# Norm products in bank pairs of their own, and a shared end of the last convolution chunk: four layers on one Trainium2 core

## The chip, the cores and the metric

One core of a Trainium2 chip runs the whole program. The metric is the device time of one execution in microseconds (us). The engines are called PE (TensorE's matrix products; PEld are its weight loads), DVE (VectorE), ACT (ScalarE), POOL (GpSimd) and SP (which here only issues transfers).

## The reference

The input is x of shape 4 x 256 x 56 x 56 in 32-bit floats. Four layers follow, each of the form x = x + layer(gn(x)); gn is a normalization over 32 groups of eight channels.

- Layer 0 is an involution: a 1x1 product to 64 channels and a second one to 49 x 16 make a 7x7 kernel for each pixel and each group of 16 channels, and that kernel is applied to the group.
- Layer 1 is a residual block of two 3x3 convolutions with batch norms and relu.
- Layer 2 is an involution again, with batch norms and relu inside.
- Layer 3 multiplies gn(x) with the sum of two gates: one per channel (a sigmoid of a 256x256 product; the sum over the transformed plane is the first pixel), and one per pixel (the real part of the 2-D Fourier transform of the channel mean, the "map" below).

## The kernel before

Work goes by units: an image b and a block cb of 128 channels, eight units in each involution. Layer 3 is fused into layer 2's involution; layer 1 runs between, in 12 chunks of 16 to 20 rows. The order on each engine is the order in which the Python code emits instructions (`in_order` fixes it). Work for other units is hung into the loops as generators, advanced at numbered places: `hooks` (after round n of the tap stage) and `late` (after column tx).

A unit has a tap stage and seven columns.

- `tap_matrices`: 32 rounds, each with six products (L613) into one pair of PSUM banks, read by DVE (L634, two rounds of three) or ACT (L627) into `kt`.
- `apply`, one call for each column: 20 + 36 products (L659) into two pairs, which ACT (L672 or L674) and DVE (four L679) sum; POOL (L684, layer 0) or DVE (L686, layer 2) adds the sum onto the image. After it, seven transposes (L427) make the next windows in a third pair, ACT copies them (L439), and SP shuffles them by transfers (L445, L446). POOL (L412) or ACT (L410) normalizes the next strip.

The pairs come from one pool of four, in rotation: a new pair waits until the readers of the one four allocations before are done. There is also `spare[0]`, a free part of a pair that is in use. It was set in the tap stage and in `apply`, where the second pair uses only its first bank:

```
pair = two_banks()
spare[0] = pair[:, 1, :]
```

`norm_steps` makes the factors of a group norm from statistics, in nine steps: the aggregate (L215), a product with a group-averaging matrix (L226), a copy and three small operations (L229 to L237), a second product (L240), the root (`rsqrt_eps`: L150 on DVE, L151 on POOL) and the shift (L244). In layer 0 the next image's norm runs between columns, its products into `spare[0]`; so does one norm in layer 2's first unit (the last image's).

`bottleneck` is the 1x1 product: first a small product (L467) whose result becomes a bias `hb` (L478 in layer 2, on DVE), then L489 into several pairs, which ACT reads with that bias (L508) into `hp`, with copies on DVE (L497). For layer 2's first image it stands in front of everything, so PE's first L613 there needs all L508.

The convolutions work on transformed columns, in the order k = 1, 2, 3, 4, 0, 5 (`KS`). `filtered_product` makes an inner and an outer pair of products (L1606) and DVE sums them (L1618 to L1624); L1810 to L1813 and `middle` (L1633, L1634) mix the columns. `joined` ends a chunk: L1752 adds the scaled result onto the normed residual. In the last chunk (i = 11), DVE also does relu and the residual sum (L1757) for both channel blocks, then SP stores them. In the chunk before it (i = 10), ACT does the relu (L1764) and a transfer on POOL accumulates the residual (L1765) before the store (L1766). The statistics of the last image are DVE's `bn_stats` (L1784), six for each of these two chunks: those of chunk 10 stand inside chunk 11, those of chunk 11 at hook 3 of layer 2's first tap stage. For earlier images they are ACT's passes over the chunk (`mean_of`, `spread_of`: L1771, L1772, L1777, L1778).

After the last column, the last image's end follows: `warm` issues idle products (L340) while DVE finishes; `last_mean` makes channel means by 28 products (L913) with the last norm between them; `last_gates` makes the map (L939, L949, L952) with DVE's L947 between, spreads it into rows (L962), and for each of seven chunks multiplies it back to all partitions (L972), followed by two L975 on DVE, two L976 on ACT and two stores. `last_ones` (L852) makes the constant tables for this with reductions of an identity matrix.

Of the kernel before, what the change touches and what calls it, by code (L numbers as in the profile page):

```python
# [12 lines left out]
ALU = mybir.AluOpType  # L13
# [60 lines left out]
def net_kernel(  # L74
# [243 lines left out]
    def involution_layer(layer, xin, xout, red, span, sb, xs_of, ahead=None, pending=None):  # L318

        with ExitStack() as es:  # L320
# [130 lines left out]
            def bottleneck(b):  # L451
# [23 lines left out]
                if layer == 0:  # L475
                    nc.vector.tensor_add(hb, ps[:, 0:1], by_row(L0_RB))
                else:
                    nc.vector.scalar_tensor_tensor(hb, ps[:, 0:1], bn["s3"], bn["t3"], ALU.mult, ALU.add)  # L478
                yield
# [166 lines left out]
            def apply(b, cb, kt, tx, xw):  # L646
# [3 lines left out]
                for ng, tys, nty, rows in O_PARTS:  # L650
                    pair = two_banks()
                    spare[0] = pair[:, 1, :]
                    nb, m = len(tys), ng * GC
                    v = pair[:, :nb, : ng * nty * TP].rearrange("p i (e n) -> p i e n", e=ng)
                    for i in range(nb):
                        for k in range(nty):
                            ty = tys[i] + k
                            for j in range(P // m):
                                nc.tensor.matmul(  # L659
                                    v[m * j : m * j + m, i, :, k * TP : (k + 1) * TP],  # L660
                                    xw[:, window(ty), m * j : m * j + m],
                                    kt[:, ng * j : ng * j + ng, :, ty * NTX + tx, :],
                                    start=True,
                                    stop=True,
                                )
                    n = rows // nb * TX
                    o = [v[:, :, e, :n] for e in range(ng)]
                    un = work.tile([P, 2, O_PARTS[0][3] // 2 * TX], F32, name="un")
                    un = un.rearrange("p i n -> p (i n)")[:, : rows * TX]
                    part = un.rearrange("p (i n) -> p i n", i=nb)  # L670
                    if layer == 0:
                        nc.scalar.mul(part, o[0], bn["par"][ng][:, 0:1])  # L672
                    else:
                        nc.scalar.activation(  # L674
                            part, o[0], AF.Identity, bias=bn["t4"][:, cb : cb + 1], scale=bn["s4"][ng][:, 0, cb : cb + 1]
                        )
                    for e in range(1, ng):
                        s = bn["par"][ng][:, e : e + 1] if layer == 0 else bn["s4"][ng][:, e, cb : cb + 1]
                        nc.vector.scalar_tensor_tensor(part, o[e], s, part, ALU.mult, ALU.add)  # L679
                    dst = img[:, y0 : y0 + rows, tx * TX : (tx + 1) * TX]  # L680
                    y0 += rows
                    u = un.rearrange("p (r x) -> p r x", x=TX)
                    if layer == 0:
                        nc.gpsimd.tensor_tensor(dst, u, dst, ALU.add)  # L684
                    else:
                        nc.vector.scalar_tensor_tensor(dst, u, 0.0, dst, ALU.max, ALU.add)  # L686
# [160 lines left out]
            def last_ones():  # L847

                by = ident_sb[:, : CR * CR]
                for i, axes in enumerate(("p (j r) -> p r j", "p (j r) -> p j r")):  # L850
                    last_xn[i] = dead(B - 1, NB - 1, 6 * CR * W + 128 + i * CR, CR)
                    nc.vector.tensor_reduce(last_xn[i], by.rearrange(axes, r=CR), mybir.AxisListType.X, ALU.add)  # L852

# [80 lines left out]
            def last_gates(b):  # L934
# [13 lines left out]
                ps = one_bank()  # L948
                nc.tensor.matmul(ps[:H, :W], half, cs2_sb, start=True, stop=False)  # L949
                for i in range(4):  # L950
                    e, c = divmod(i, 2)
                    nc.tensor.matmul(  # L952
                        ps[:H, :W], down[: H // 2, e, c], part[:, e, c], start=False, stop=(i == 3)
                    )

# [4 lines left out]

                rows = dead(b, NB - 1, 2 * CR * W, CR * W)[:H]
                nc.vector.tensor_tensor(  # L962
                    rows.rearrange("y (r w) -> y r w", r=CR),
                    ps[:H, :W].unsqueeze(1).to_broadcast([H, CR, W]),
                    last_xn[0][:H].unsqueeze(2).to_broadcast([H, CR, W]),
                    ALU.mult,
                )
                nc.vector.scalar_tensor_tensor(back, shift, -1.0, inv, ALU.mult, ALU.mult)
                for j in range(NCHUNK):
                    at = slice(j * CR * W, (j + 1) * CR * W)  # L970
                    sf = one_bank()[:, : CR * W]
                    nc.tensor.matmul(sf, last_xn[1][:H, j : j + 1].to_broadcast([H, P]), rows, start=True, stop=True)  # L972
                    for cb in range(NB):
# [14 lines left out]
            def norm_of(layer, sts, u0, u1):  # L988
                return norm_steps(sts, lambda: spare[0], layer, u0, u1)

            hooks0 = {}
            if layer == 0:
                place(hooks0, begin(), (1, 2, 4, 6, 7))
            else:
# [4 lines left out]
                run(bottleneck(0))  # L999
                hooks0[3] = list(pending[0])  # L1000
                for _ in range(NXW - 1):
                    next_windows()
                    next_strip()
                hooks0[7] = [next_windows, next_strip]
            if layer == 0:
                next_strip()
# [36 lines left out]
            for u, (b, cb) in enumerate(units):  # L1043
# [24 lines left out]
                if b + 1 < B:  # L1068
                    n = 16 if layer == 0 else (26, 21)[cb]
                    hooks.setdefault(n, []).append(load_step(b + 1, cb))  # L1070

                last_image = layer == 0 and b == B - 1
                if last_image and cb == 0:
# [11 lines left out]
                if b + 1 < B:  # L1085
                    if layer == 0:
                        g = sums(b + 1, cb)
                        if cb == 0:
# [3 lines left out]
                            def norm_first():  # L1092
                                yield from norm_of(0, {u + 2: sums_of[b + 1, 0]}, u + 2, u + 3)

                            g = norm_first()
                            for tx in (3, 4, 4, 4, 4, 4, 5, 5, 6):
                                late[tx].append(step(g))
                        else:
# [3 lines left out]
                            def norm_last():  # L1102
                                yield from norm_of(0, {u + 2: sums_of[b + 1, 1]}, u + 2, u + 3)

                            g = norm_last()
                            late[1].append(step(g))
                            late[2] += [step(g)] * 5
                            late[3] += [step(g)] * 3
# [15 lines left out]
                if last_image and cb == 0:  # L1124
                    g = norm_of(1, {}, 0, u)
                    for tx in (1, 2, 2, 2, 2, 2, 3, 3, 4):
                        late[tx].append(step(g))
                if layer == 2 and u == 0:
                    g = norm_of(2, dict(enumerate(pending[1], NB * (B - 1))), NB * (B - 1), NB * B)
                    for tx in (1, 2, 2, 2, 2, 2, 3, 3, 4):  # L1130
                        late[tx].append(step(g))
# [30 lines left out]
            if layer == 2:  # L1162
                run(last_normed(b, 0))
                bank = one_bank()
                mean, norm = last_mean(b, bank), by_counts(norm_steps({u: st}, lambda: bank, 3, u, u + 1), (1, 1, 4, 1, 1, 1))
                warm(16, ident_sb)
                for _ in range(2):
# [53 lines left out]
    def conv_layer(xin, xout, st, ahead):  # L1221
        with ExitStack() as es:
# [474 lines left out]
            def conv2(i, after, between, sums, tail):  # L1697
# [28 lines left out]
                def joined(co):  # L1726
# [28 lines left out]
                    at = slice(y0 * W, y1 * W)  # L1755
                    if i == n_chunks - 1:
                        stt(xj, rj, 0.0, xj, ALU.max, ALU.add)  # L1757
                        nc.sync.dma_start(xout[bb][co][:, at], x)
                    else:
                        added(x, xj, rj, co, at)  # L1760

                def added(x, xj, rj, co, at):

                    nc.scalar.activation(xj, rj, AF.Relu)  # L1764
                    nc.gpsimd.dma_start(x, xin[bb][co][:, at], accum_op=ALU.add)  # L1765
                    nc.sync.dma_start(xout[bb][co][:, at], x)  # L1766

# [12 lines left out]
                def stats(co, k):  # L1780

                    r0, r1 = k * ST_ROWS, min(n, (k + 1) * ST_ROWS)
                    at = sum(ST_PIECES[: i % 3]) + k
                    nc.vector.bn_stats(sums[co][:, at, :], xr_of[i, co][:, r0 * W : r1 * W])  # L1784

# [43 lines left out]

                if not summed or bb == B - 1:  # L1830
                    tail += [[lambda co=co, k=k: stats(co, k) for k in range(ST_PIECES[i % 3])] for co in range(NB)]
# [59 lines left out]
            for s, (conv, i) in enumerate(order):  # L1891
# [47 lines left out]
                else:  # L1939
                    if i % 3 == 0:  # L1940
                        sums_of[i // 3] = [
                            work.tile([P, 3, 3], F32, name="st3", bufs=4)
                            if i // 3 < B - 1
                            else small.tile([P, sum(ST_PIECES), 6], F32, name=f"st_c{co}", bufs=1)
                            for co in range(NB)
# [4 lines left out]
                    if late_v is not None:  # L1950
                        place(after, late_v, (0,) if i < n_chunks - 1 else ())
                        late_v = None
                    loads_at = (2, 4) if i < n_chunks - 1 else (4, 7)
                    for at, fs in zip(loads_at, tail2):
                        for k, f in enumerate(fs):
                            after[at - (k == 0)].append(f)
                    tail2 = []
# [138 lines left out]
```

## Time and profile before

| | us |
|---|---|
| median of three runs | 1666.82 (1665.92 to 1667.41) |
| the profiled execution, its own time | 1665.74 |
| its span in the profile | 1663.7 |
| taps and columns of layer 0 | 46 to 504 |
| the convolutions | 504 to 1124 |
| layer 2 (with layer 3) | 1124 to 1631 |
| the last image's end | 1631 to 1664 |

The span runs from the first to the last instruction; the times in the profile count from its start. In a line of a time line stand the start, the length, the engine, the source line, the operation, what is written and read, and in brackets the idle time of the engine before it with what ended it. Matrix products are recorded twice each, as two passes. PEclk is the clock that was granted to TensorE, as a share of the full one.

### The profile page before, as it was taken

The numbers are of one execution on the slowest core, as the hardware profiler recorded it, in microseconds if no ns is written. First come the engines' busy times: TensorE is split into PE (matmuls) and PEld (weight loads), VectorE is DVE, ScalarE is ACT, GpSimd is POOL, SyncE is SP. The second block draws the span as 40 slices with busy tenths as digits, with TensorE's granted clock in tenths as the row PEclk, the third lists the DMA queues.
The fourth block names the chain that finished last, engine by engine and source line by source line (L and its number), as shares of the span: only waits on it lengthen the run. The fifth ranks groups of instructions, "written<-read, shape, count | busy, mean of one in ns | idle before, by whom it ended". The sixth has DMA issues, their size and how long they took to land.

```text
span 1663.7 us, 57362 instructions
## 1 busy us (share of the span) xinstructions
PE 1586.3 (95%) x24600; PEld 1442.0 (87%) x24600; DVE 1328.1 (80%) x2391; ACT 1010.6 (61%) x2203; POOL 552.1 (33%) x764
## 2 busy tenths in 40 slices
PE   6999999999989999999999999988999899899998
PEld 4997998898888898899999999976888888788886
DVE  2686887787659988899999999987777678678775
ACT  1655655557446565666666567426677577577565
POOL 2133223322522343423333333200000662662671
PEclk9999999999999999999999999998999999999997
DMA  2363445444558977987788797744445765764753
GB/s 92 111 197 115 157 155 169 146 156 132 181 171 266 171 130 150 198 174 157 159 166 170 163 197 151 172 144 145 131 140 166 216 220 188 210 216 159 206 168 113
DMA packets 102875, 275.67 MB, mean 166 GB/s; under 512 B 15877, under 2 KB 43790, under 8 KB 98910
## 3 DMA queue, kind: packets, MB, share of 16 engines
q0 software_dynamic: 43856, 106.25, 31.3%
q1 hardware_dynamic: 57726, 164.48, 30.7%
q8 instruction: 195, 3.19, 0.8%
q10 hardware_dynamic: 1040, 1.26, 0.3%
q14 instruction: 58, 0.48, 0.1%
HBM read 95.07 MB, written 49.15 MB: 87 GB/s over the span
## 4 chain that ended last, share of the span: by engine, by line
PE 68%; DVE 13%; DMA 6%; issue 6%; ACT 4%; SPq 1%; POOL 1%; ACTq 0%; POOLq 0%; DVEq 0%
PE ps L613 21%; PE mm L1606 17%; PE ps L659 15%; PE mm L1591 6%; DVE un L679 3%; PE ps L427 3%; DMA xw<-xw 2%; DVE kt L634 2%; PE ps L489 2%; DMA xs<-x 1%; ACT hp L508 1%; DMA xs<-v 1%; SPq L445 1%; DVE st L380 1%; ACT xs L1737 1%
## 5 line engine op out<-in xcount | busy, mean ns | idle before, releaser
L659 PE MATMUL ps<-kt,xw 126*32 126x48 f32 (+1 forms) x12544 | 378.9, 235 | 23.1 <-DMA xw<-xw 9.6
L659 PEld LDWEIGHTS ps<-kt,xw 126*32 126x32 f32 (+1 forms) x12544 | 340.9, 121 | 66.3 <-issue 40.4
L613 PE MATMUL ps<-hp,z_sb 64*126 64x133 f32 x6144 | 376.0, 278 | 1.8 <-ACT hp L508 0.9
L613 PEld LDWEIGHTS ps<-hp,z_sb 64*126 64x126 f32 x6144 | 364.1, 186 | 13.1 <-DVE kt L634 6.0
L634 DVE TENSOR_TENSOR kt<-ps,zb_sb 126x798 f32<-126x798 f32 x352 | 331.9, 980 | 48.9 <-PE ps L613 29.8
L627 ACT ACTIVATE kt<-ps,zb_sb 126x133 f32<-126x133 f32 x960 | 280.5, 441 | 78.1 <-PE ps L613 78.1
L1606 PE MATMUL mm<-xs,u_sb 128*128 128x140 f32 (+2 forms) x1664 | 210.3, 279 | 4.2 <-DMA xs<-v 4.1
L1606 PEld LDWEIGHTS mm<-xs,u_sb 128*128 128x128 f32 x1664 | 200.8, 192 | 4.6 <-issue 4.5
L1591 PE MATMUL mm<-v,u_sb 128*128 128x280 f32 (+2 forms) x864 | 193.9, 383 | 2.4 <-DVE hp L1622 1.7
L1591 PEld LDWEIGHTS mm<-v,u_sb 128*128 128x128 f32 x864 | 161.6, 189 | 28.0 <-PE mm L1606 2.2
L684 POOL TENSOR_TENSOR xs<-un,xs 128x240 f32<-128x240 f32 x112 | 72.0, 663 | 298.8 <-DVE un L679 298.7
L679 DVE SCALAR_TENSOR_TENSOR un<-ps,s,un 128x240 f32<-128x240 f32 x224 | 102.5, 458 | 85.2 <-ACT un L674 79.2
L679 DVE SCALAR_TENSOR_TENSOR un<-ps,par_sb,un 128x240 f32<-128x240 f32 x224 | 97.7, 456 | 84.3 <-ACT un L672 80.2
L1574 POOL DMA_DIRECT2D xs<-v x100 | 96.6, 1003 | 182.8 <-ACT xs L1573 161.7
L672 ACT ACTIVATE un<-ps,par_sb 128x240 f32<-128x240 f32 x112 | 50.2, 448 | 131.8 <-PE ps L659 121.0
L439 ACT COPY xw<-ps 126x896 f32<-126x896 f32 x112 | 101.3, 905 | 39.8 <-PE ps L427 22.0
L427 PE MATMUL ps<-ident_sb,strip_sb 128*126 128x128 f32 x784 | 112.7, 285 | 5.2 <-POOL strip_sb L412 2.0
L674 ACT ACTIVATE un<-ps,bn_t,s 128x240 f32<-128x240 f32 x112 | 60.1, 538 | 92.3 <-PE ps L659 85.2
L427 PEld LDWEIGHTS ps<-ident_sb,strip_sb 128*126 128x126 f32 x784 | 85.8, 142 | 16.1 <-POOL strip_sb L412 3.7
L1606 PE MATMUL mm<-v_sb,u_sb 128*128 128x140 f32 (+2 forms) x688 | 95.2, 281 | 3.2 <-ACT u_sb L1353 1.8
L1606 PEld LDWEIGHTS mm<-v_sb,u_sb 128*128 128x128 f32 x688 | 88.4, 193 | 4.3 <-ACT u_sb L1353 2.0
L1573 ACT ACTIVATE xs<-v 128x560 f32<-128x560 f32 (+2 forms) x100 | 61.8, 629 | 44.3 <-DVE v L1518 35.9
(325 smaller groups left out, 2344.2 us busy)
## 6 DMA issues: line engine op xcount, KB each, us to landing
xw<-xw SPq DMA_DIRECT2D x224, 252.0 KB
xw<-xw SPq DMA_DIRECT2D x224, 126.0 KB
xs<-x POOLq DMA_DIRECT2D x24, 560.0 KB, 6.9
x<-xs POOLq DMA_DIRECT2D x8, 1568.0 KB, 8.1
xs<-x SPq DMA_DIRECT2D x8, 1568.0 KB
xs<-v POOLq DMA_DIRECT2D x44, 280.0 KB, 4.3
xs<-v POOLq DMA_DIRECT2D x42, 252.0 KB, 4.2
xs<-in_x_dram SPq DMA_DIRECT2D x6, 1568.0 KB
```

What stands on the lines that cost most here:

```text
L427: nc.tensor.transpose(ps[:Q, k * P : (k + 1) * P], flat[:, k * Q : (k + 1) * Q], ident_sb)
L439: nc.scalar.copy(xw[:, :NSB, :], ps[:Q, : NSB * P].rearrange("q (n c) -> q n c", n=NSB))
L613: nc.tensor.matmul(ps[:Q, i, k * NT : (k + 1) * NT], z_sb[i * R : (i + 1) * R, cb * GB // 2 + gp, z0 : z0 + Q], hp[i * R : (i + 1) * R, py ...
L627: nc.scalar.activation(kt[:, g0 + i, pb, :, k], ps[:Q, i, k * NT : (k + 1) * NT], AF.Identity, bias=zb_sb[:, cb * GB + g0 + i, p0 + k : p0 ...
L634: nc.vector.tensor_tensor(kt[:, g0 : g0 + 2, pb], ps[:Q, :, : PB * NT].rearrange("q i (k t) -> q i t k", k=PB), zb_sb[:, cb * GB + g0 : cb ...
L659: nc.tensor.matmul(v[m * j : m * j + m, i, :, k * TP : (k + 1) * TP], xw[:, window(ty), m * j : m * j + m], kt[:, ng * j : ng * j + ng, :, ...
L679: nc.vector.scalar_tensor_tensor(part, o[e], s, part, ALU.mult, ALU.add)
L684: nc.gpsimd.tensor_tensor(dst, u, dst, ALU.add)
L1573: nc.scalar.mul(t[:, at], v[:, below], -1.0)
L1574: nc.gpsimd.dma_start(t[:, at], v[:, at], accum_op=ALU.add)
L1591: nc.tensor.matmul(ps, *position(u, v, ci, dy, k, co, n), start=(j == 0), stop=(j == NB * 3 - 1))
L1606: nc.tensor.matmul(ps[:, bank, co * m : (co + 1) * m], u[ci][:, co * P : (co + 1) * P], v2[:, : n // 2, ci * WT : (ci + 1) * WT], start=(c ...
```

## The change

1. `hb` in layer 2 is made by ACT in place of DVE, four times.
2. `apply` no longer sets `spare[0]`. The norms that run between columns take a pair from the pool for each of their two products (`norm_between`, in six groups of steps). For the units with cb = 0, and in the two single norms, the second product and what follows stand one or more columns later than before; for cb = 1 the order is the same.
3. In the last convolution chunk the end is shared: channel block 0 goes as in chunk 10 (relu on ACT, residual by an accumulating transfer), block 1 stays on DVE. Chunk 10's statistics become ACT's passes, placed in chunk 11's last product, ahead of the new relu. The last chunk's two stores and six statistics are spread over hooks 3, 5, 7 and so on of layer 2's first tap stage; the stores come first.
4. At the end, nine idle products stand in place of 16; the map is made on partitions 0 to 55 and 64 to 119, and the chunks' products use the two halves in turn.

The diff, cut to its core:

```diff
@@ bottleneck
-                    nc.vector.scalar_tensor_tensor(hb, ps[:, 0:1], bn["s3"], bn["t3"], ALU.mult, ALU.add)
+                    nc.scalar.activation(hb, ps[:, 0:1], AF.Identity, bias=bn["t3"], scale=bn["s3"])
@@ apply
-                    spare[0] = pair[:, 1, :]
@@ last_ones
-                    nc.vector.tensor_reduce(last_xn[i], by.rearrange(axes, r=CR), mybir.AxisListType.X, ALU.add)
+                    nc.vector.tensor_reduce(last_xn[i], ident_sb.rearrange(axes, h=2, r=CR), mybir.AxisListType.XY, ALU.add)
@@ last_gates
-                nc.tensor.matmul(ps[:H, :W], half, cs2_sb, start=True, stop=False)
-                for i in range(4):
-                    e, c = divmod(i, 2)
-                    nc.tensor.matmul(
-                        ps[:H, :W], down[: H // 2, e, c], part[:, e, c], start=False, stop=(i == 3)
-                    )
+                halves = [slice(h * R, h * R + H) for h in range(2)]
+                for at in halves:
+                    nc.tensor.matmul(ps[at, :W], half, cs2_sb, start=True, stop=False)
+                    for i in range(4):
+                        e, c = divmod(i, 2)
+                        nc.tensor.matmul(
+                            ps[at, :W], down[: H // 2, e, c], part[:, e, c], start=False, stop=(i == 3)
+                        )
...
+                for at in halves:
+                    nc.vector.tensor_tensor(
+                        rows[at].rearrange("y (r w) -> y r w", r=CR),
...
-                    nc.tensor.matmul(sf, last_xn[1][:H, j : j + 1].to_broadcast([H, P]), rows, start=True, stop=True)
+                    sf, of = one_bank()[:, : CR * W], halves[j % 2]
+                    nc.tensor.matmul(
+                        sf, last_xn[1][of, j : j + 1].to_broadcast([H, P]), rows[of], start=True, stop=True
+                    )
@@ the units
+            def norm_between(layer, sts, u0, u1):
+                return by_counts(norm_steps(sts, one_bank, layer, u0, u1), (1, 1, 4, 1, 1, 1))
...
-                hooks0[3] = list(pending[0])
...
+                for n, f in enumerate(pending[0]):
+                    hooks0.setdefault(3 + 2 * n, []).append(f)
...
+                if layer == 0 and cb == 1 and b + 1 < B:
+                    place(hooks, first, (5,))
...
-                            for tx in (3, 4, 4, 4, 4, 4, 5, 5, 6):
+                            for tx in (3, 4, 5, 6, 6):
...
-                    g = norm_of(2, dict(enumerate(pending[1], NB * (B - 1))), NB * (B - 1), NB * B)
-                    for tx in (1, 2, 2, 2, 2, 2, 3, 3, 4):
+                    g = norm_between(2, dict(enumerate(pending[1], NB * (B - 1))), NB * (B - 1), NB * B)
+                    for tx in range(1, 7):
...
-                warm(16, ident_sb)
+                warm(9, ident_sb)
@@ conv2
-                    if i == n_chunks - 1:
+                    if i == n_chunks - 1 and co == 1:
                         stt(xj, rj, 0.0, xj, ALU.max, ALU.add)
-                        nc.sync.dma_start(xout[bb][co][:, at], x)
+                        tail.append([lambda: nc.sync.dma_start(xout[bb][co][:, at], x)])
...
+                if i == n_chunks - 2:
+                    for f in (mean_of, spread_of):
+                        tail.append([lambda co=co, f=f: f(sums[co][:, 2 * ST_PIECES[0]], xr_of[i, co][:, : n * W]) for co in range(NB)])
+                elif bb == B - 1:
                     tail += [[lambda co=co, k=k: stats(co, k) for k in range(ST_PIECES[i % 3])] for co in range(NB)]
...
-                    loads_at = (2, 4) if i < n_chunks - 1 else (4, 7)
-                    for at, fs in zip(loads_at, tail2):
+                    for at, fs in zip((2, 4), tail2):
                         for k, f in enumerate(fs):
-                            after[at - (k == 0)].append(f)
+                            after[at - (k == 0) if i < n_chunks - 1 else 10].append(f)
```

## Prediction

> **What bounds the kernel now.** I read the page first, then TensorE's waits, then the time lines of the places that the diff touches, then the windows of the tail. Page, busy time (engine, us, share of the span, instructions):
>
> ```profile
> PE 1586.3 (95%) x24600; PEld 1442.0 (87%) x24600; DVE 1328.1 (80%) x2391; ACT 1010.6 (61%) x2203; POOL 552.1 (33%) x764
> ```
> ```profile
> PE ps L467 <- DVE hp L1624: 5.2, 1, 5.2
> PE ps L226 <- DVE un L679: 4.9, 7, 1.0
> PE ps L240 <- DVE un L679: 4.4, 8, 1.0
> ```
>
> PE is the bound nearly everywhere, so what can be won are PE's own gaps. The second fence is from TensorE's waits over the whole span (us, times, longest): the products of the norm chain wait 9.3 us for L679, and the entry to the last layer waits 5.2 us for VectorE. The time line of PE at one such product:
>
> ```profile
> 205.02 3.27 PE L659 MATMUL ps<-kt,xw 126*64 126x96 f32 x112
> 208.22 0.98 PE L427 MATMUL ps<-ident_sb,strip_sb 128*126 128x128 f32 x7
> 209.70 0.38 PE L226 MATMUL ps<-mv_sb,gavg_sb 128*128 128x1 f32 x2 [0.50 <-DVE un L679]
> 210.01 3.27 PE L659 MATMUL ps<-kt,xw 126*64 126x96 f32 x112
> ```
>
> A column is 4.1 us of PE; the product adds 0.31 of work and 0.50 of wait. L226 needs only `mv_sb`; it waits because it writes the second bank of the pair that L679 still reads. Next, the seam between the convolutions and the last layer (PE, DVE, ACT):
>
> ```profile
> 1117.31 2.07 PE L1606 MATMUL mm<-u_sb 128*128 128x140 f32 x16
> 1124.54 1.01 PE L467 MATMUL ps<-norm_sb,red_sb 128*128 128x1 f32 x4 [5.16 <-DVE hp L1624]
> ...
> 1141.47 7.82 PE L613 MATMUL ps<-hp,z_sb 64*126 64x133 f32 x96 [0.85 <-ACT hp L508]
> ```
> ```profile
> 1109.92 0.63 DVE L1784 BATCH_NORM_STATS2 st_c<-u_sb 128x6 f32<-128x448 f32 x1 [3.43 <-DMA u_sb<-x]
> ...
> 1129.46 2.27 DVE L1757 SCALAR_TENSOR_TENSOR xs<-u_sb,xs 128x1120 f32<-128x1120 f32 x1
> ...
> 1147.43 2.78 DVE L1784 BATCH_NORM_STATS2 st_c<-xs 128x6 f32<-128x448 f32 x6
> ```
> ```profile
> 1108.59 2.43 ACT L1718 ACTIVATE u_sb<-xs,shift,norm_sb 128x1120 f32<-128x1120 f32 x1
> 1133.29 8.34 ACT L508 ACTIVATE hp<-ps,hb,bn_s 64x168 f32<-64x168 f32 x20 [22.27 <-DVE hb L478]
> ```
>
> VectorE stands still 3.43 us for a transfer that only its statistics need, is then late to the end, and ScalarE idles 22 us until VectorE has made `hb`. Last, the tail:
>
> ```profile
> 1631.47 3.84 PE L340 MATMUL ps<-ident_sb 128*128 128x128 f32 x32
> 1635.15 1.46 PE L913 MATMUL ps<-gavg_sb,xs 128*112 128x16 f32 x14
> 1647.36 10.82 PE L972 MATMUL ps<-xs 56*128 56x448 f32 x14 [0.71 <-DVE xs L962]
> ```
>
> **Norm products.** 15 waits, 9.3 us, go. What is late next: a product now takes a turn in the rotation of four pairs, so the next column's first pair is the first pair of this column, free at its third L679. In layer 2 such a column starts at 1177.08 and its third L679 ends at 1181.39; without the wait PE would arrive at 1181.58. Margin 0.2. In the three units with cb=1, where L380 loads VectorE, the third L679 of one column ends at 141.1 and PE would arrive at 140.96; replayed, these units keep about 0.3 of their 1.35 us each. Gain 9.3 - 0.9 = 8.4; bounds 4.2 (half comes back) and 9.3. L240 and `rsqrt_eps` go one column later, POOL's L151 behind one more L684/L412 pair (and in the last image behind the L369 copies); their reader is the bottleneck a unit later, so this costs nothing; without that unit of cover it would cost about one column, 4.1. L150 waits for L240 with L634 behind it, but L240 stands on PE before the products that L634 reads.
>
> **The seam.** Replay with the rows' durations. Six L1784 and the DMA wait leave VectorE, so the first L1618 starts when L1808 ends (1106.5) and not at 1110.46. PE's k=0 products then follow the k=4 ones without the 1.34 us stall and k=5 ends at 1117.9. VectorE runs L1810 to L1813 from 1111.0, k=0's four sums to 1116.1, L1633/L1634 to 1117.4, k=5's four to 1119.8. That is L1624's end, 4.7 earlier, and L467 follows it.
> ScalarE now has the statistics of the chunk before: two of 1.12 + 0.19 + 0.20 (L1771, L1772) and two of 0.19 + 1.23 + 0.19 (L1777, L1778), 6.2 us, in front of `hb`. They wait for that chunk's stores; these were issued at 1109.95 and 1112.66, and the DMA share is 0.24 from 1114 to 1118 and 0.01 after, about one busy us, so they land near 1115. ScalarE is done at about 1120, before L467 ends at 1120.8: hidden. Queued behind this wait are `hb` and L508, and PE's last L489 and L613 wait for those, so every us beyond would go straight into the path. Behind `hb` stands the new L1764 (2.28), from L1752's end at 1121.2 to 1123.5, then L508's 8.2 to 1131.9; I take 1132.4 for the first L613, as PE's clock may be halved once more while it waits. 1141.47 - 1132.4 = 9.1, taken as 9.0. `z_sb` (issued 1133.5, packets gone by 1138, so 4.5) can go once L1757 ends at 1124.8, the two SP stores no longer standing before it: ready about 1131. Bounds 4.7 (only L1624's gain stays) and 10.
> POOL's new accumulating transfer stands before L391 and L412: 0.88, and L391 now at 1125, 7 earlier than before. The two stores move on SP behind the `cs`, `z_sb` loads and eight xw issues (about 1139 by then); their accumulation, 7.2 us, lands at 1132, so nothing queues behind them (nor behind the first L1784, two rounds later on VectorE); were it late, the third window's L445 would wait, with cover until the first column.
>
> **Spread statistics.** Six L1784 behind every second round in place of 2.78 us in one lump, which cost PE 0.40 + 0.48. Per six rounds VectorE then has 4 x 0.92 + 3 x 0.46 = 5.1 against 4.4 of PE: about 1.3 over the twelve rounds, part of it taken by the buffers. Net 0, bounds -0.9 and +0.9.
>
> **The tail.** Seven idle products fewer are 14 x 0.112 = 1.57 us, and L913's rows are ready: the last L686 ends at 1633.39, the shorter row of products at 1633.48. Against it stands the clock. The windows view:
>
> ```profile
> 1638.00:1640.00 2.00, 2.00 (x23) 2.00 (x22) 0.59 (x3) 0.50 (x1) 0.56 (x1) 1.00 0.00 0
> 1640.00:1642.00 2.00, 2.00 (x16) 2.00 (x16) 0.00 (x0) 0.91 (x2) 0.00 (x0) 0.65 0.00 0
> ```
>
> (The third last number is the granted clock.) It fell at 1640.6, 5.5 us after the last dense product, and L913 went from 0.098 to 0.187 each. If it falls as late after the products again, it eats little; if 2 us earlier, L913 loses 2 x 0.91 more, all that is won. I take 1.1, bounds -0.3 and 1.6. The Trainium skill ("TensorE: Matmul & The Clock Gate", Part 1) speaks against the cut: PE's busy-ness is judged in free-running windows of about 3.4 us, so a shorter burst may leave the window before L913 quiet; by it the fall could come 3.4 us after the products, and this term would be -0.3 us instead of 1.1.
> The map: five more products, ten instructions at 0.093 (L952's pace), 0.9 us, beside the first L962 (0.62); the second L962 ends at 1648.3 and holds up only j=1. L972 takes 0.75 per instruction, 1.5 per chunk, while L975's pair takes 1.21. Two halves of PE's rows do work side by side: L613's 64-row pairs step at 0.061 per 133 columns, L1606's full ones at 0.12 per 140. So VectorE sets the pace: 1649.26 + 14 x 0.605 + 0.07 = 1657.8 against 1659.49. Of 1.7 I take 1.4, the output transfers being 0.9 busy there; bounds 0 and 1.7.
>
> **Edits at nothing.** `hb` on ScalarE in the other three images (0.2 less on DVE, 0.2 more on ACT, in its idle 0.3 to 1.8 before L674): 0 +- 0.6. The wider L852, 0.1, lies beside L613.
>
> **Sum.** 8.4 + 9.0 + 0 + 1.1 + 1.4 = 19.9. The profiled execution took 1665.74 (span 1663.7, 2.04 around it): 1645.8. The median of the three runs is 1.08 above it: 1647.0 rounded.
>
> **Rivals.** (1) ScalarE becomes the bound at the seam: if stores land at 1119 and not 1115, statistics end near 1125, L508 starts near 1128 and the seam gives 4.8: 1651. For it: ScalarE has 6.2 us more, in order, before `hb`; against: a DMA share of 0.01 after 1118. Chance 0.17.
> (2) The rotation returns the wait: 0.5 at each of 16 products leaves the norm part nothing: 1655.3. For it: a margin of only 0.2. Chance 0.10.
> (3) The slower side, by the same rotation: with a wait w at each of the 16 products the total gain is 20.8 - 16w, nothing at w = 1.3. With w = 2.0 (PE arriving before L674 and its three L679, 0.55 + 1.47) it is 11 slower, 1678. Against it: the release rows above lie within 0.2 of PE's arrival. Chance 0.04.
> (4) The change does less than it says: halves don't overlap, clock falls early: -0.3 for the tail in place of 2.5: 1649.7; inside my range.
>
> **How the numbers follow.** The forecast as worked out, with (4), 0.66; (1) 0.17; (2) 0.10; within 0.2% (3.3 us, about what a measurement can tell from no change) 0.03; (3) 0.04. So faster 0.93, same 0.03, slower 0.04. The range: all upper bounds, 9.3 + 10 + 0.9 + 1.6 + 1.7 = 23.5, give 1643.3, and 0.9 for the spread of the runs 1642.4; upwards it reaches past (1) and (2), to 1656.
>
> **What would show it.** Right: no L226 or L240 waiting for L679; L467's wait under 2.5; L508 starting within 9 us of the last block of L1606 (it was 16), L613 about 16 after it (it was 24); DVE back to back in L975. Wrong: a new wait of L659 for L679 after a product; `hb` waiting behind L1778; the clock falling before L913 is half done.

## The result, and the profile after

| kernel | median of its runs, us | ratio to before, 95% interval |
|---|---|---|
| before (4 runs) | 1666.37 (1664.09 to 1667.41) | |
| changed (4 runs) | 1646.16 (1639.85 to 1648.03) | 0.9874 [0.9846, 0.9902] |
| changed, measured again (6 runs) | 1646.72 (1640.60 to 1653.05) | 0.9878 [0.9848, 0.9908] |

Each ratio is to before as it was measured beside that kernel (a median of 1665.83 for the last row). The forecast was 1647.0 (1642 to 1656). The profiled execution of the changed kernel was the fastest of its four, 1639.85, with a span of 1637.3. So the two profiles differ by 26 us and the medians by 20, and no stage may be read from this pair alone. That matters below.

The page, busy time (engine, us, share, instructions), and TensorE's waits over the span (us, times, longest):

```profile
PE 1574.1 (96%) x24596; PEld 1435.3 (88%) x24596; DVE 1324.4 (81%) x2381; ACT 1020.4 (62%) x2220; POOL 555.8 (34%) x767
```
```profile
PE ps L658 <- DVE un L678: 5.5, 14, 1.2
...
PE ps L467 <- DVE hp L1634: 2.0, 1, 2.0
```

L226 and L240 no longer wait for the columns' sums (9.3 us before). But a line has grown: the columns' own products, L658, wait 5.5 us for L678, where before had 2.5:

```profile
PE ps L659 <- DVE un L679: 2.5, 5, 0.8
```

The entry to the last layer waits 2.0 in place of 5.2.

PE's time line in unit (0,1), where the statistics load VectorE, shows where that line comes from:

```profile
138.24 0.28 PE L226 MATMUL ps<-mv_sb,gavg_sb 128*128 128x1 f32 x2
138.99 3.27 PE L658 MATMUL ps<-kt,xw 126*64 126x96 f32 x112 [0.48 <-DVE un L678]
```

The product itself goes at once; the next column pays 0.48. That this is because the product took a turn in the four pairs is read from the code here, and tested below (`norm_windows`).

The seam (PE, then DVE, then ACT):

```profile
1104.38 2.07 PE L1616 MATMUL mm<-u_sb 128*128 128x140 f32 x16
1108.47 0.60 PE L467 MATMUL ps<-norm_sb,red_sb 128*128 128x1 f32 x4 [2.02 <-DVE hp L1634]
1109.00 7.62 PE L489 MATMUL ps<-xs,redn 128*64 128x504 f32 x28
...
1121.24 1.03 PE L613 MATMUL ps<-hp,z_sb 64*126 64x133 f32 x13 [1.43 <-DMA z_sb<-z_dram]
```
```profile
1107.17 1.23 ACT L1792 ACTIVATE u_sb<-u_sb,c 128x1120 f32<-128x1120 f32 x1
1108.31 0.19 ACT L1792 ACTIVATION_READ_ACCUMULATOR u_sb<-u_sb,c 128x1 f32 x1
1109.11 0.35 ACT L478 ACTIVATE hb<-ps,bn_t,bn_s 128x1 f32<-128x1 f32 x1 [0.62 <-PE ps L467]
1109.87 2.26 ACT L1774 ACTIVATE xs<-u_sb 128x1120 f32<-128x1120 f32 x1 [0.40 <-DVE u_sb L1762]
1112.37 8.35 ACT L508 ACTIVATE hp<-ps,hb,bn_s 64x168 f32<-64x168 f32 x20 [0.23 <-PE ps L489]
```

From the last block of L1616 to L508 it is now 8.0 us (16.0 before), to the first L613 16.9 (24.2 before). ScalarE ends its statistics at 1108.5 and then still waits 0.62 for L467: the cover that the prediction named is there, but it is thin. What the first L613 waits for last is now the load of `z_sb`, 1.43; L508 ends at 1120.7, half a microsecond before that product starts.

The tail:

```profile
1618.04 0.92 PE L937 MATMUL ps<-xs 112*28 112x224 f32 x2 [0.24 <-DVE xs L929]
...
1621.75 1.28 DVE L963 TENSOR_TENSOR xs<-ps,xs 56x448 f32<-56x448 f32 x2 [2.03 <-PE ps L952]
...
1622.42 7.45 PE L973 MATMUL ps<-xs 56*128 56x448 f32 x14 [0.71 <-DVE xs L963]
```

L973's 14 instructions take 7.45 us (10.82 before): the halves of PE's rows do overlap. But the first row product, L963, starts 3.71 after the gates' first product; before it was 2.41 (1646.69 after 1644.28):

```profile
1644.28 0.92 PE L939 MATMUL ps<-xs 112*28 112x224 f32 x2 [0.24 <-DVE xs L931]
...
1646.69 0.62 DVE L962 TENSOR_TENSOR xs<-ps,xs 56x448 f32<-56x448 f32 x1 [0.74 <-PE ps L952]
```

### The profile page after: what moved, and what is told of

The parts are those of the page before. It is cut to its first block, busy times and chain, and to the rows that moved or that the text cites. A ratio compares the mean times of both kernels' runs of the same rounds, so it can differ in the third digit from the quotient of the medians.

```text
span 1637.3 us, 57397 instructions
## 1 busy us (share of the span) xinstructions
PE 1574.1 (96%) x24596; PEld 1435.3 (88%) x24596; DVE 1324.4 (81%) x2381; ACT 1020.4 (62%) x2220; POOL 555.8 (34%) x767
## 4 chain that ended last, share of the span: by engine, by line
PE 75%; DVE 10%; DMA 5%; ACT 4%; issue 3%; POOL 1%; SPq 1%; ACTq 0%; POOLq 0%; DVEq 0%
PE ps L613 21%; PE mm L1616 20%; PE ps L658 15%; PE mm L1601 9%; PE ps L427 4%; DVE un L678 3%; DMA xw<-xw 3%; DVE kt L634 2%; PE ps L489 2%; DMA xs<-v 1%; DMA xs<-x 1%; PE ps L741 1%; DVE st L380 1%; SPq L445 1%; PE ps L292 1%
## 5 line engine op out<-in xcount | busy, mean ns | idle before, releaser
L658 PE MATMUL ps<-kt,xw 126*32 126x48 f32 (+1 forms) x12544 | 377.9, 235 | 24.7 <-DMA xw<-xw 8.9
L658 PEld LDWEIGHTS ps<-kt,xw 126*32 126x32 f32 (+1 forms) x12544 | 339.5, 121 | 70.0 <-issue 42.1
L613 PE MATMUL ps<-hp,z_sb 64*126 64x133 f32 x6144 | 374.5, 277 | 3.2 <-DMA z_sb<-z_dram 1.4
L613 PEld LDWEIGHTS ps<-hp,z_sb 64*126 64x126 f32 x6144 | 362.0, 185 | 14.5 <-DVE kt L634 5.9
L1616 PE MATMUL mm<-xs,u_sb 128*128 128x140 f32 (+2 forms) x1664 | 209.4, 278 | 2.1 <-DMA xs<-v 2.1
L1616 PEld LDWEIGHTS mm<-xs,u_sb 128*128 128x128 f32 x1664 | 200.2, 191 | 2.4 <-issue 1.5
L678 DVE SCALAR_TENSOR_TENSOR un<-ps,s,un 128x240 f32<-128x240 f32 x224 | 102.5, 458 | 81.3 <-ACT un L673 75.0
L678 DVE SCALAR_TENSOR_TENSOR un<-ps,par_sb,un 128x240 f32<-128x240 f32 x224 | 98.0, 456 | 77.5 <-ACT un L671 73.4
L1616 PE MATMUL mm<-v_sb,u_sb 128*128 128x140 f32 (+2 forms) x688 | 93.7, 278 | 1.9 <-ACT u_sb L1363 1.9
L1616 PEld LDWEIGHTS mm<-v_sb,u_sb 128*128 128x128 f32 x688 | 86.8, 190 | 2.9 <-ACT u_sb L1363 2.1
```

Of the source, the lines that this page charges most:

```text
L613: nc.tensor.matmul(ps[:Q, i, k * NT : (k + 1) * NT], z_sb[i * R : (i + 1) * R, cb * GB // 2 + gp, z0 : z0 + Q], hp[i * R : (i + 1) * R, py ...
L658: nc.tensor.matmul(v[m * j : m * j + m, i, :, k * TP : (k + 1) * TP], xw[:, window(ty), m * j : m * j + m], kt[:, ng * j : ng * j + ng, :, ...
L1616: nc.tensor.matmul(ps[:, bank, co * m : (co + 1) * m], u[ci][:, co * P : (co + 1) * P], v2[:, : n // 2, ci * WT : (ci + 1) * WT], start=(c ...
```

## Experiments

### The parts, each alone

`norm_only` is before with part 2 of the change, `seam_only` with parts 1 and 3, `tail_only` with part 4; their diffs are those pieces of the change.

> The kernel before with the norm products' change alone (part 2 of the change: own pairs, one group of steps for each column). Theory A, the term of the prediction: the 9.3 us that L226 and L240 wait for L679 go, 0.9 comes back: 8.4 less, so 1658.0 against 1666.4, a ratio of 0.995; the columns' products wait under 1 us for DVE's reads of their pairs. Theory B, read from the trace of the changed kernel: the products' turns in the rotation give the wait back, 5.5 us of waits of the columns' products for DVE stand where 2.5 stood and the layer-0 units are only 3.5 us shorter: 9.3 - 3.0 - 0.9 - 1.5 = about 4 less, 1662.4, a ratio of 0.9976.

Measured: 1657.49, ratio 0.9957 [0.9937, 0.9976].

> The kernel before with the shared end of the last chunk alone (parts 1 and 3 of the change). Theory A, the prediction: 9.0 less, 1657.4, a ratio of 0.9946; the stage from the convolutions' start to L467 is 4.7 shorter, L467 to the first L613 4.3. Theory B: the trace of the changed kernel shows 9.35 in the convolutions, 4.2 up to L613 and 2.3 in the first tap stage; if all of it belongs to the change, 15.8 less, 1650.6, a ratio of 0.9905. What of the 9.35 goes beyond 4.7 should then stand in the last chunks and not in those before chunk 10.

Measured: 1654.14, ratio 0.9939 [0.9916, 0.9962].

> The kernel before with part 4 of the change alone (nine idle products for 16, the map on both halves). Theory A, the prediction: 2.5 less, 1663.9, a ratio of 0.9985: 1.1 up to the gates and 1.4 after them. Theory B, read from the trace of the changed kernel: the clock falls during L913 and takes the 1.1 back, the output transfers at full share take the 1.4: within 0.5 us of before.

Measured: 1664.77, ratio 0.9991 [0.9966, 1.0016].

Taken on the 1665 to 1666 of before, that is 7.2, 10.2 and 1.5 us less, 18.9 together, each with about 3 to 4 us on either side. Within these intervals the parts add up to the whole (20 to 21), but such times can't tell the theories apart. The traces can, since most stages in which PE waits neither for a transfer nor for something that the profile doesn't show (`issue`) repeat within 0.1 us. So here are the stage lengths (between PE's first instructions of successive stages) over all 14 profiles of this study, before and after among them: for the columns, 5 profiles without the norm part, 5 with it, 4 of `norm_windows` and what is built on it (below); median, us. The units (0,0), (1,0) and (2,0) have such waits in some of the profiles of each group, so the sum of the shortest ones stands beside that of the medians.

| stage | without | with | norm_windows |
|---|---|---|---|
| columns of (0,0) | 30.82 | 30.30 | 30.57 |
| columns of (0,1) | 36.95 | 36.07 | 35.84 |
| columns of (1,0) | 31.22 | 29.53 | 29.59 |
| columns of (1,1) | 36.96 | 36.10 | 35.58 |
| columns of (2,0) | 31.40 | 30.95 | 31.15 |
| columns of (2,1) | 36.97 | 36.17 | 35.86 |
| columns of (3,0) | 30.40 | 29.84 | 29.52 |
| columns of layer 2's first unit | 31.04 | 29.56 | 29.19 |
| sum of these | 265.76 | 258.52 | 257.30 |
| the same sum of the shortest ones | 263.42 | 257.29 | 253.29 |
| columns of layer 2's last unit | 29.50 | 31.29 | 30.96 |

| stage | without the seam part | with it |
|---|---|---|
| convolutions to L467 (4 and 10 profiles) | 603.9 | 599.1 |
| L467 to the first L613 (3 without both pieces, 9 with both) | 16.90 | 12.65 |
| first tap stage of layer 2 (4 and 10) | 27.7 | 27.2 |

The profile of before has 609.9 in the convolutions, 6 us over three other profiles with the same code there; the 9.35 that the first pair of profiles showed in that stage was half such spread. So for the seam theory A holds in both places: 4.9 and 4.25 measured, 4.7 and 4.3 expected. For the norm products it lies between the theories' 8.4 and 4: 6.1 to 7.2 in the units, less 1.7 of new waits in the last unit (below).

### Where the norm part's missing us went

`norm_windows` puts the products where no turn is needed (its diff, cut to its core):

```diff
@@ begin_windows
+                spare[0] = ps[:, NSB * P :]
@@ next_windows: between the transposes and ACT's copy
+                for f in mid:
+                    f()
@@ norm_between
-                return by_counts(norm_steps(sts, one_bank, layer, u0, u1), (1, 1, 4, 1, 1, 1))
+                return by_counts(norm_steps(sts, lambda: spare[0], layer, u0, u1), (1, 1, 4, 1, 1, 1))
```

> The changed kernel, but each of the two norm products goes into the last 128 columns of the pair that holds the seven transposes (L427), between them and ACT's copy (L439), so that it takes no turn in the rotation. Theory B (the rotation is the price): the waits of the columns' products for DVE fall from 5.5 us to about 2.5 as before the change, and L226 and L240 wait for nothing: 3 to 4 less than the changed kernel, 1642 to 1643, a ratio to before of about 0.986. Rival: ACT's copy then waits for the product and for DVE's sums behind it, the next windows come later, and it is within 1 us of the changed kernel, 1646, ratio 0.988.

Measured: 1645.50, ratio 0.9885 [0.9857, 0.9913]; the time alone decides nothing. TensorE's waits over the span and the same place of unit (0,1):

```profile
PE ps L661 <- DVE un L681: 3.1, 10, 0.4
```
```profile
141.10 0.28 PE L226 MATMUL ps<-mv_sb,gavg_sb 128*128 128x1 f32 x2
141.31 1.30 PE L661 MATMUL ps<-kt,xw 126*64 126x96 f32 x21
142.84 2.24 PE L661 MATMUL ps<-kt,xw 126*64 126x96 f32 x91 [0.23 <-issue]
```

The wait of 0.48 behind L226 is gone, and the columns of (1,1) fall from 36.10 to 35.58. So the turn in the rotation was a part of the price, as theory B had it, but not all of it: in the four kernels without the turn the eight units of the table still wait 2.1 to 3.0 us for L681, against 3.1 to 3.6 for L678 with it. And the unit shown is no shorter, 36.08: it has a wait that the profile puts down to nothing (`issue`). Of the 12 units with cb = 1 in these four kernels, the seven without such a wait take 35.56 to 35.60, the five with one 36.07 to 36.21. Where it comes from stays open. ACT's copy behind the product costs nothing that the seven show.

The last unit shows a second price that nobody had asked for. In all five profiles with the norm part, its columns wait 1.7 us for L678, in none of the nine others. In the changed kernel:

```profile
PE ps L658 <- DVE un L678: 1.7, 3, 1.2
```

This stage has no norm product. But the changed `apply` no longer renews `spare[0]`, and the last image's gate products (L771, after the columns) write there: they now hold a pair of the last tap round through all seven columns, which leaves three pairs to rotate. `norm_windows` renews it each column, and has no such wait (its stage is hardly shorter, 30.96: it waits longer for the windows' transfers there, so what the 1.7 cost in the end can't be read from the lengths). That the held pair is the cause is read from the code and this contrast; a version that renews it and changes nothing else was not run.

### The seam's two pieces

`hb_only` is before with `hb` on ACT; `seam_no_hb` is `seam_only` with `hb` left on DVE. The diff of the first, which is left out of the second:

```diff
-                    nc.vector.scalar_tensor_tensor(hb, ps[:, 0:1], bn["s3"], bn["t3"], ALU.mult, ALU.add)
+                    nc.scalar.activation(hb, ps[:, 0:1], AF.Identity, bias=bn["t3"], scale=bn["s3"])
```

> The kernel before with hb on ACT alone (part 1 of the change). Theory A (hb behind VectorE's L1757 is the whole wait of the seam): L508 starts some 7 us earlier, right after the first L489, and the stretch from L467 to the first L613 falls from 16.9 to about 12.7, what the whole shared end gives there: 4.2 less, ratio 0.9975. Theory B (the second L1757, on VectorE, also holds the strips and z_sb's load, which come after it): L508 is early, but L613 then waits for z_sb or the strip, and the stretch falls by 2.5 at most. In both the convolutions' stage up to L467 stays as before (604 to 610).

Measured: 1658.76, ratio 0.9956 [0.9936, 0.9975]; L467 to L613 takes 13.38, the convolutions 603.7. ScalarE there:

```profile
1119.70 0.35 ACT L478 ACTIVATE hb<-ps,bn_t,bn_s 128x1 f32<-128x1 f32 x1 [14.53 <-PE ps L467]
1123.60 0.87 ACT L508 ACTIVATE hp<-ps,hb,bn_s 64x168 f32<-64x168 f32 x2 [3.55 <-DVE u_sb L1752]
```

`hb` is ready at 1120.05, yet L508 waits 3.55 more for the second L1752. Both theories had a part wrong: `hb` was not all of the wait (A), and what L613 waits for last is L508, 0.51, and not `z_sb` or the strip (B). Moving `hb` alone is worth 3.5 us of the seam's 4.25, more than B's 2.5.

> The kernel before with part 3 of the change alone (hb stays on VectorE). Theory A: hb then stands behind L1767 and the strip's fill (1113.4 and 1114.7 on the changed kernel's clock, where L508 began at 1112.4), so L508 and the first L613 come 2.4 later than with hb on ACT: L467 to L613 takes 15 to 15.3. Theory B: z_sb, which L613 waited 1.4 for in the changed kernel, and the strip cover a part, and it is 13.5 to 14. In both the convolutions' stage keeps its gain of 4 (about 600), so the ratio is about 0.995 to 0.996.

Measured: 1660.36, ratio 0.9965 [0.9942, 0.9988]; the convolutions 598.2, L467 to L613 14.55.

```profile
1120.83 0.20 DVE L404 MEMSET strip_sb<- 128x168 f32 x1 [1.08 <-POOL strip_sb L391]
1120.94 0.10 DVE L478 SCALAR_TENSOR_TENSOR hb<-ps,bn_s,bn_t 128x1 f32<-128x1 f32 x1
```

`hb` stands behind the strip's fill, as theory A said, and costs 1.9 (14.55 against 12.65), between A's 2.4 and B's 1. So in the stretch behind L467 either piece alone gives 2.4 to 3.5, and both together 4.25: they shorten the same wait. The 4.9 in the convolutions belongs to the other piece, the statistics and the shared end.

`lumped` is the changed kernel with `hooks0[3] = list(pending[0])` again:

> The changed kernel with the last chunk's two stores and statistics in one lump at hook 3 of the first tap stage again, as before the change. The prediction's term for the spreading was 0, within 0.9. Theory A: PE's waits in the first tap stage (0.6 when spread) rise to 0.9 to 1.5, as before the change, the stage is 25.6 to 26.5 at full clock. Rival: the lump, 2.8 us of VectorE, now meets PE at a fuller pace and costs over 1.5.

Measured: one run, 1652.90. The waits in that stage (27.73 long, with 3.9 us of it at half clock):

```profile
PE ps L613 <- DVE kt L634: 0.5, 1, 0.5
PE ps L427 <- ACT kt L627: 0.4, 1, 0.4
```

0.9 in place of 0.6 in the changed kernel: the spreading is worth 0.3 in waits, theory A. The 6 us of its time lie elsewhere (layer 2's units that wait for window transfers), and one run says nothing on them.

### The map

`half_stores` cuts the last image's 14 stores to half their columns (`xs[:, : CR * W // 2]`).

> The changed kernel, but each of the last image's 14 stores writes only the first half of its columns (the second half of the last image's output is left out), so the output transfers at the end are halved. If their rate sets the end (DMA share 1.00 over the last 8 us), the end comes earlier: from the last L979 to the end falls from 3.9 to about 2.5 or less, and gates to end by 1.0 or more. If VectorE's pace and the late first L963 set it, gates to end falls by under 0.6, what a smaller last transfer saves by itself.

Measured: one run; gates to end 18.12, against 19.26 in the changed kernel. The windows view of the changed kernel and of `half_stores` (last three numbers: granted clock, DMA share, GB/s):

```profile
1628.00:1630.00 2.00, 1.87 (x3) 0.49 (x2) 2.00 (x4) 2.00 (x5) 0.00 (x0) 0.50 1.00 374
1630.00:1632.00 2.00, 0.00 (x0) 0.00 (x0) 2.00 (x4) 2.00 (x4) 0.00 (x0) 0.50 0.99 376
```
```profile
1634.00:1636.00 2.00, 0.00 (x0) 0.00 (x0) 2.00 (x5) 2.00 (x4) 0.00 (x0) 0.50 0.55 189
```

With VectorE at its new pace the DMA share is 1.00; with half the bytes it is 0.55, and the end comes 1.14 earlier. From the last ACT instruction to the end it is 3.9 in the changed kernel, 3.5 before, 2.75 with half the bytes.

`windows_wide` and `windows_banks` go at the late L963; both are built on `norm_windows`, and their diffs are cut to the core. The first lays the tables twice side by side, so that five products make both halves and one L963 makes all rows:

```diff
-                for at in halves:
-                    nc.tensor.matmul(ps[at, :W], half, cs2_sb, start=True, stop=False)
...
+                nc.tensor.matmul(ps[:, :W], last_xn["half"], cs2_sb, start=True, stop=False)
...
```

> norm_windows with the map's tables laid twice side by side (two times 64 columns), so that one set of five products makes both halves, and one L963 over all 128 partitions makes the rows. Theory A (the map's gain of 1.4 was lost to the second set of products, for which even the first L963 waited): the first L963 starts 1.3 us earlier after the gates' first product (2.4 as before the change, not 3.7), and the stretch from there to the end falls from 19.3 to 17.9 or 18.0. Theory B (output transfers at full share set the end, whatever comes before): it stays over 19. Time: that of norm_windows less 1.3 or less nothing, ratio to before about 0.987 to 0.988.

Measured: 1640.48, ratio 0.9824 [0.9801, 0.9848]; the last stretch 19.42.

```profile
1625.75 1.95 PE L963 MATMUL ps<-xs 28*128 28x56 f32 x8
...
1627.74 0.62 DVE L971 TENSOR_TENSOR xs<-ps,xs 128x448 f32<-128x448 f32 x1 [1.77 <-PE ps L963]
```

A miss for theory A. Eight instructions with 128 columns of weights take 1.95, with 56 columns they took 0.99 (L952): the five wide products cost nearly as much as the ten narrow ones, and L971 still starts 3.44 after the gates' first product (at 1624.30). The stretch stays over 19, as theory B said; but as the rows came hardly earlier, this run can't decide for it.

The second keeps the ten products and only gives each half its own pair:

```diff
-                ps = one_bank()
+                maps = [one_bank() for _ in halves]
-                for at in halves:
+                for ps, at in zip(maps, halves):
...
```

> norm_windows with the map's two halves in two pairs of banks instead of one, nothing else changed in the map. Theory A (the first L963 waited for the second half's products only because both halves stood in one tile): it starts 2.4 after the gates' first product instead of 3.7, the second one at 3.7, and L973 at 3.7 instead of 4.4, so the last stretch is 0.5 to 0.7 shorter than 19.26. Rival (output transfers): they start 0.7 earlier too and run at the same rate, so 0.3 or less is seen at the end. Time: 1644 to 1645, ratio 0.987.

Measured: 1643.99 (1640.39 to 1645.88), ratio 0.9862 [0.9837, 0.9888]; the last stretch 18.46.

```profile
1619.46 0.92 PE L940 MATMUL ps<-xs 112*28 112x224 f32 x2 [0.24 <-DVE xs L932]
...
1621.88 0.62 DVE L966 TENSOR_TENSOR xs<-ps,xs 56x448 f32<-56x448 f32 x1 [0.75 <-PE ps L955]
...
1622.14 0.99 PE L955 MATMUL ps<-xs 28*56 28x56 f32 x8
...
1623.06 5.43 PE L976 MATMUL ps<-xs 56*128 56x448 f32 x12
```

Theory A: the first row product starts 2.42 after, beside the second half's products, and L976 at 3.60; the stretch is 0.80 shorter. The late start was a matter of one tile for both halves. That not all of the 1.29 is won fits the rival: the end is 0.80 earlier, and what follows VectorE's last instruction still takes 4.6. The Trainium skill ("Perfetto Trace Analysis", Optimizing Tensor Performance) has independent groups of products rotate through different banks so that the reading of one overlaps the next; these rows agree, 2.42 against 3.71.

### Two repeats

> The changed kernel once more, beside the three below. Expected 1646 and a ratio to before of 0.987 to 0.988 if its first four runs were typical.

Measured: 1646.72, ratio 0.9878, as expected.

> windows_wide once more. Its six runs were 5 us faster than those of norm_windows, but in its profile the last stretch was no shorter (19.4), so no step of it accounts for that. If the 5 us were the spread of the runs, it is now 1644 to 1646 like the others (ratio 0.987); if they belong to the kernel, 1640 (0.982 to 0.984).

Measured: 1643.97, ratio 0.9863 [0.9837, 0.9889]. The 5 us were spread; the first six runs of `windows_wide` were lucky. `windows_banks`, the best of the versions by its steps, is 1643.99 beside 1646.72 of the changed kernel on the same chip; their intervals overlap, and it is its waits and stages, not its time, that say it is faster.

## Why the prediction was right, point by point

**Norm products: 8.4 predicted, 6.1 to 7.2 in the units, less 1.7 in the last one.** The mechanism held: L226 and L240 wait for no sums. Mis-sized was "0.9 comes back". In the eight units L658 and L489 now wait 3.1 for L678, where there was nothing of the kind (3.1 to 3.6 in the five profiles): 9.3 less 3.1 is 6.2, close to the 6.1 that the shortest stages show. Gaps under 0.15 us, which this view leaves out, add about 1, so the balance is no better than that. The replay had the units with cb = 1 win 1.05 of their 1.35 each; measured are 0.88, 0.86 and 0.80, and with the turn taken away (`norm_windows`) up to 1.4. So the margin of 0.2 did not hold: layer 2's first unit, on which it was worked out, waits 0.5. And a step was missing: who else uses `spare[0]`. Rival (2) was thus right in kind, at two fifths of its price; rival (3) had the price wrong.

**The seam: 9.0 predicted, 9.1 measured** (4.9 in the convolutions, 4.25 behind them). Both halves of the sum held, though `z_sb`, which the sum had ready 1.4 before L613, came last there; and L508 and L613 came 8.0 and 16.9 after the last block of L1616, where 9 and 16 were said. Rival (1) fell: ScalarE waited 0.62 for `hb`'s product. It was close: in `seam_only` it did not wait, and began `hb` 0.2 after that product had ended.

**Spread statistics: 0 predicted, 0.3 in waits.** The stage's length moves by 3 us with the clock, more than any statistics do.

**Idle products: 1.1 predicted; on average 1.4, in the first pair of profiles 0.06.** The working was right. Over all 14 profiles the stretch from the first idle product to the gates is a constant and half of the time that it spends at half clock:

```
           stretch   at half clock   stretch less half of that
16 idle    12.80     3.69            10.96
           13.81     5.83            10.90
           15.17     8.70            10.82
           15.21     8.78            10.82
           13.15     4.42            10.94
9 idle     13.12     7.65             9.29
           12.74     6.87             9.31
           11.44     4.11             9.38
           12.17     5.66             9.34
           10.91     2.99             9.41
           13.83     8.84             9.41
           13.40     8.27             9.27
           13.94     9.38             9.25
           12.04     5.39             9.35
```

The means of the last column are 10.89 and 9.33: 1.56, where 14 products of 0.112 were 1.57. The means of the middle one are 6.3 and 6.6, so the earlier fall of the clock that the Trainium skill's rule ("TensorE: Matmul & The Clock Gate", Part 1, free-running windows) warned of costs 0.14 on average, not the 1.4 that would have made this term -0.3. The stretch less the whole time at half clock is the time to the fall: 6.4 to 9.1 us with 16 idle products, 4.6 to 7.9 with nine, on average 1.7 earlier. So the clock does fall earlier, by about what the burst is shorter, and the gates come nearly as much earlier. What the rule gets right besides is the scatter: within each group the moment of the fall spreads by 2.7 and 3.4 us, no more than one of its windows.

**The map: 1.4 predicted, 0.14 measured** (medians 19.40 and 19.26). This is the step that failed. VectorE set the pace as said, back to back: its 14 instructions take 10.23 in L975 before and 8.38 in L978, 1.85 less. But "beside the first L962" was wrong: the first row product waited for both halves' products, 1.30 (five more products, priced at 0.9), and behind VectorE's last instruction, with the output transfers at a share of 1.00, 0.4 of the rest was given back. Rival (4) was right that the map gains little and wrong on the reason: the halves do overlap, and the gain was lost on both sides of them.

**The signs.** All four signs of being right were seen. Of the three of being wrong, the first was seen too, the new wait of the columns' products behind a norm product (0.48 at 138.99), and it told what the norm term lost. `hb` did not wait behind the statistics. The clock fell before L913 was half done in two of the nine profiles with nine idle products and in two of the five with 16, so that sign says nothing on the change.

**The sum.** 7.2 (medians of the units), less 1.7 (the last unit's wait, taken whole), 9.1, 0.3, 1.4 and 0.1 make 16.4; the ratio says 21.0, from 16.3 to 25.7, and the second measurement 20.3. So the forecast of 19.9 came close partly because what the steps lost was made up elsewhere. By the stage medians some 4 us lie in (3,1) and in layer 2's later units, whose PE waits for window transfers and whose lengths spread by 2 to 5 us from run to run. Whether that is more than spread stays open.

## What to carry to other kernels

A buffer that is lent for free is never only one line: before it is taken away, look for every later reader of the name, and count what its replacement takes out of a rotation. Where work is doubled so that a later step runs on two halves, give each half its own bank, or the first half waits for the second. And where single profiles spread by more than the change, read the same stage in all profiles that share its code: medians of short stages settled here to some tenths of a microsecond what whole times left open by 4.

## What the runs showed of the hardware

A short stall can cost more than its length. In the profile of before, PE waited 2.39 us for a transfer in the middle of the convolutions, and the clock then fell for one stretch of 3.41 us:

```profile
690.83 3.27 PE L1606 MATMUL mm<-xs,u_sb 128*128 128x140 f32 x16 [2.39 <-DMA xs<-v]
```
```profile
690.00:692.00 2.00, 1.17 (x8) 1.20 (x9) 1.97 (x4) 1.97 (x7) 0.00 (x0) 0.92 1.08 300
692.00:694.00 2.00, 2.00 (x10) 2.00 (x10) 1.43 (x2) 2.00 (x5) 0.27 (x1) 0.50 0.99 320
694.00:696.00 2.00, 2.00 (x14) 2.00 (x13) 1.39 (x2) 0.00 (x0) 1.47 (x2) 0.73 0.55 115
```

Half of 3.41, an estimate of what it cost, is 1.7 us on top of 2.4. It happened again at 742.9 after a wait of 1.74, and these two make up most of the 6 us by which before's convolutions were longer than the same code in three other profiles. Ahead of the last image's end, all stretches at half clock last 3.41, 6.83 or 10.24 us. But such a wait need not cost this: of the 20 waits of 1.6 to 2.6 us that PE has in the convolutions of the 14 profiles, four were followed by a stretch at half clock and 16 were not, two longer ones among them (2.48 at the same place in `seam_only`, 2.59 in `tail_only`). This was read in the traces and not tried.

The other surprise was that products of 28 rows and 56 moving columns took 0.12 us per pass with 56 columns of weights and 0.24 with 128, at half clock (0.99 and 1.95 for eight, above): in these two rows the time goes with the width of the weights.
